# A projection whose sum stays on chip: three of four windows of x1 are kept for the next layer, the first part of x is loaded in the last attention head, and the last two outputs get buffers of their own

## The chip, the core and the metric

The kernel runs on one core of a Trainium2 chip. The core has five engines that run beside each other, each with its own instruction queue: PE (matmuls, with weight loads shown as PEld), DVE (vector work), ACT (pointwise functions and copies), POOL and SP. In this kernel SP does nothing but issue transfers (DMAs); ACT and POOL issue some too. An engine works through its queue in order: an instruction that waits holds back all that stand behind it. Tiles live in the on-chip memory (SBUF, 128 partitions) or in the matmul output memory (PSUM); `dram.tile` is scratch in the chip's main memory. The metric is the time of one execution on the device, in microseconds (us).

## What is computed

One image of 48 channels, 256 x 256, float32, goes through two layers. Cut to what matters:

```python
# layer 0: attention over 4x4 patches, 8 heads, then a 48x48 projection, added to x
qkv = dwconv3x3(einsum('bchw,oc->bohw', gn(x), w_qkv), w_dw)
q, k, v = (heads(unfold4x4(t)) for t in split(qkv, 3))        # 8 heads, 96 x 4096 (+ border)
attn = softmax(einsum('bhcn,bhcm->bhnm', l2norm(q), l2norm(k)) * temperature)
out = fold4x4(einsum('bhcn,bhnm->bhcm', v, attn))
x1 = x + einsum('bchw,oc->bohw', out, w_proj)
# layer 1: on windows of 64 x 64, a sum of three products over width, height and channel
y = gn(x1)                                # group norm: 16 groups of 3 channels, over the whole image
result = x1 + sum_t einsum('bchw,wW,hH,cC->bCHW', window(y), Ws[t], Hs[t], Cs[t])
```

The group norm of x1 needs a mean and a variance over the whole image, so layer 1 cannot begin with a window before the last row of x1 is known.

## The kernel before

**Attention (lines 521 to 715, up to 3318 us of the span).** Heads are worked one after the other, each in 16 steps `g` of two blocks of 128 queries. A step computes two blocks of scores (L344), their exponentials on ACT (L563), and four groups of weighted sums, `weigh` (L592), which DVE adds to `oacc` (L603); meanwhile DVE and ACT prepare the next head (depthwise convolution, in the pool `cv`). In the last head there is no next one, so DVE and ACT have less to do there. In the last step of a head, `store(h, m)` turns the finished sums: PE transposes (L609) into a PSUM tile `pt` (two buffers), ACT copies that into `oo` (L611, two buffers), and POOL writes `oo` with two DMAs (L613) to the scratch `os_`. So the copy of `m` has to wait until both DMAs of `m - 2` have landed. The order of the instructions on every engine is the order of the program text here (`tc.manual_schedule()`).

**Projection (L722 to L781).** x1 is made in eight tiles of 16 rows from the upper and 16 rows from the lower half of the image: channels of the upper half in partitions 0 to 47, of the lower half in 48 to 95. For each tile SP loads two pieces of `os_` (`pot`, L733) and two of x (`pxt`, L734), 768 KB each. PE multiplies by `wp`, a 96 x 96 matrix with `w_projT` twice on its diagonal (L739, eight matmuls of 512 columns in four PSUM tiles `pps`, three buffers). DVE adds the four PSUM tiles to `pxt` (L746) and takes statistics of each pair of rows (`bn_stats`, L750, eight times). POOL writes the tile to the scratch `x1s` (L755). `pot` and `pxt` have three buffers each, so a load of x waits until the write of the tile three before has landed. A scheduler, not the text, orders this part. Then `group_stats` (L761) and a second chain for a 112-partition copy of the variance (`rstd2`, L762 to L767) scale the matrix `csn` (L775); `cbias` (L781) holds what the mean contributes.

**Layer 1 (L784 to L916), in the text's order.** There are eight units: four windows of 64 rows (`yw`) by two halves of the columns (`xh`). For a unit, SP loads `lxq` (L808), the 48 channels of 32 rows in partitions 0 to 47 and of the other 32 rows in 64 to 111, and `lrt` (L817), the same values with rows in the partitions. Both come from `x1s`. `over_c` (L834) multiplies by `csn` in 11 steps of up to three rows, each of which DVE moves from PSUM (`pa`, two buffers) to `lzt` (L841). `over_w` (L856) and `over_h` (L873) do width and height; ACT copies between them (L863), DVE adds the result to `lrt` (`residual`, L885), POOL writes it to the output (L888). The over_c of unit 0 runs alone; the over_c of unit u + 1 is spread over unit u, two steps after each `over_w`, and `over_h` follows after both `over_w` of a third of the unit (`q`).

Every DMA instruction of SP and ACT carries one of eight semaphores in turn and waits, before it is issued, until the DMA that used the same one before it (eight DMAs earlier on the two queues together) has landed. DMAs of POOL have eight others.

Of the kernel before, what the change touches and what calls it, by code (L numbers as in the profile page):

```python
# [16 lines left out]
C = 48  # L17
# [27 lines left out]
def conv_preact_kernel(  # L45
# [36 lines left out]
    make_identity(nc, ident)  # L82
    ones = const.tile([C, 128], F32, name="ones")
# [9 lines left out]
    wp = const.tile([P2, P2], F32, name="wp")  # L93
    nc.vector.memset(wp, 0.0)
    for s in range(2):
        r = slice(s * C, (s + 1) * C)
        for h in range(NH if s == 0 else H0):
            o = s * M0 + h * HC if h < H0 else (h - H0) * HC
            nc.scalar.dma_start(
                out=(wq[r] if h < H0 else wr[0:C])[:, o : o + HC].rearrange("c (z e) -> c z e", z=3),  # L100
                in_=w_qkvT.rearrange("c (z h e) -> h c z e", z=3, h=NH)[h],
            )
        nc.scalar.dma_start(out=wp[r, r], in_=w_projT)
# [22 lines left out]
    mean1 = const.tile([P2, 1], F32, name="mean1")  # L126
    rstd1 = const.tile([P2, 1], F32, name="rstd1")
# [7 lines left out]
    def group_stats(st, mean, rstd, pool, pspool):  # L135

        mv = pool.tile([P2, 2], F32, name="mv")
        nc.vector.bn_aggr(mv, st.rearrange("p n s -> p (n s)"))
        pm = pspool.tile([P2, 1], F32, name="pm", tag="pstat")
        nc.tensor.matmul(pm, lhsT=gm, rhs=mv[:, 0:1], start=True, stop=True)  # L140
        nc.vector.tensor_copy(mean, pm)
        d = pool.tile([P2, 1], F32, name="gsd")
        nc.vector.tensor_sub(d, mv[:, 0:1], mean)
        e = pool.tile([P2, 1], F32, name="gse")
        nc.vector.scalar_tensor_tensor(e, d, d, mv[:, 1:2], ALU.mult, ALU.add)
        pv = pspool.tile([P2, 1], F32, name="pv", tag="pstat")
        nc.tensor.matmul(pv, lhsT=gm, rhs=e, start=True, stop=True)
        f = pool.tile([P2, 1], F32, name="gsf")
        nc.vector.tensor_scalar_add(f, pv, EPS)
        g = pool.tile([P2, 1], F32, name="gsg")  # L150
        nc.scalar.activation(g, f, AF.Sqrt)
        nc.vector.reciprocal(rstd, g)
        return mv, e
# [255 lines left out]
    with tc.tile_pool(name="xn", bufs=1) as xnp, tc.tile_pool(name="cst", bufs=1) as cst, tc.tile_pool(  # L409
# [19 lines left out]
        group_stats(st0, mean0, rstd0, cst, nps)  # L429
# [48 lines left out]
    cv = attention.enter_context(tc.tile_pool(name="cv", bufs=1))  # L478
# [42 lines left out]
    with tc.tile_pool(name="ahead", bufs=2) as ah, tc.tile_pool(name="ae", bufs=3) as ae, tc.tile_pool(  # L521
        name="asm", bufs=6
    ) as asm, tc.tile_pool(name="ao", bufs=1) as ao, tc.tile_pool(name="big", bufs=3, space=PSUM) as big:
        MB = 8
# [80 lines left out]
        def store(h, m):  # L605
# [4 lines left out]
            oo = asm.tile([HD, 512], F32, name="oo", bufs=2)  # L610
            nc.scalar.copy(oo, pt.rearrange("p i n -> p (i n)"))  # L611
            for i in range(512 // TP):
                nc.gpsimd.dma_start(  # L613
                    out=os_[m * (512 // TP) + i, h * HD : (h + 1) * HD, :], in_=oo[:, i * TP : (i + 1) * TP]
                )
# [16 lines left out]
        with tc.manual_schedule():  # L632
            load_query(0, 1)
            block = scores(0, 0)
            for h in range(NH):
                more = h + 1 < NH
                rows = {r: Depthwise(h + 1, r) for r in range(CR + 1)} if more else {}
                for g in range(NG):
                    p, d, n = rows.get(g - 2), rows.get(g - 1), rows.get(g)

                    if h == 0 and 0 < g <= 6:
# [40 lines left out]
                    for k in range(NK):  # L682
# [28 lines left out]
                        if g == NG - 1 and k > 0:  # L711
                            for m in range(2 * k - 2, 2 * k):
                                store(h, m)
            for m in range(6, 8):
# [5 lines left out]
    RP = TP // PX * KS  # L720
    NP = TP
    with tc.tile_pool(name="pj", bufs=3) as pj, tc.tile_pool(name="pjs", bufs=1) as pjs, tc.tile_pool(  # L722
        name="pps", bufs=3, space=PSUM
    ) as pps, tc.tile_pool(name="pp1", bufs=1, space=PSUM) as pp1:
        st1 = pjs.tile([P2, HALF * W // 512, 6], F32, name="st1")
        ov = os_.rearrange("t (c k) n -> t c k n", k=KK)
        for t in range(HALF // RP):
            ot = pj.tile([P2, KK, NP], F32, name="pot")
            xt = pj.tile([P2, RP, W], F32, name="pxt")
            for s in range(2):  # L730
                r = slice(s * C, (s + 1) * C)
                y0 = s * HALF + t * RP
                nc.sync.dma_start(out=ot[r], in_=ov[s * (NT // 2 // TP) + t])  # L733
                nc.sync.dma_start(out=xt[r], in_=xc[:, y0 : y0 + RP, :])  # L734
            xv = xt.rearrange("p (py ki) (px kj) -> p ki kj py px", ki=KS, kj=KS)
            for ki in range(KS):
                ps = pps.tile([P2, KS, NP], F32, name="pps")
                for i in range(0, KS, 2):
                    nc.tensor.matmul(  # L739
                        ps[:, i : i + 2, :],  # L740
                        lhsT=wp,
                        rhs=ot[:, ki * KS + i : ki * KS + i + 2, :],
                        start=True,
                        stop=True,
                    )
                nc.vector.tensor_add(  # L746
                    xv[:, ki], ps.rearrange("p k (py px) -> p k py px", py=RP // KS), xv[:, ki]
                )
            for i in range(0, RP, 2):
                nc.vector.bn_stats(  # L750
                    st1[:, (t * RP + i) // 2, :], xt[:, i : i + 2, :].rearrange("p a b -> p (a b)")
                )
            for s in range(2):
                y0 = s * HALF + t * RP
                nc.gpsimd.dma_start(out=x1s[:, y0 : y0 + RP, :], in_=xt[s * C : (s + 1) * C])  # L755

        gm2 = pjs.tile([P2, 64 + C], F32, name="gm2")
        nc.vector.memset(gm2, 0.0)
        for o in (0, 64):
            nc.vector.tensor_copy(gm2[:, o : o + C], gm[:, 0:C])  # L760
        mv1, e1 = group_stats(st1, mean1, rstd1, pjs, pp1)  # L761
        pc1 = pp1.tile([64 + C, 1], F32, name="pc1", tag="pstat")  # L762
        nc.tensor.matmul(pc1, lhsT=gm2, rhs=e1, start=True, stop=True)
        rstd2 = l1c.tile([64 + C, 1], F32, name="rstd2")
        nc.vector.tensor_scalar_add(rstd2, pc1, EPS)
        nc.scalar.activation(rstd2, rstd2, AF.Sqrt)
        nc.vector.reciprocal(rstd2, rstd2)  # L767
# [190 lines left out]
```

## Time and profile before

| what | value |
|---|---|
| time of three runs | 3765.82, 3767.5, 3774.27 us (median 3767.5) |
| the profiled execution's own time | 3774.41 us |
| its span, first to last instruction | 3772.6 us, 100069 instructions |
| PE, DVE, ACT busy in the span | 3521.1, 2185.9, 1715.5 us (93%, 58%, 45%) |
| 0 to 3288 us (all but the end of the last head) | PE busy 3138.4 us, DMA share 0.44, 111 GB/s |
| 3288 to 3475 us (end of attention, projection, statistics) | PE busy 97.4 us, granted clock 0.69, DMA share 0.91, 221 GB/s |
| 3475 to 3773 us (layer 1) | PE busy 285.4 us, granted clock 0.95, DMA share 0.70, 123 GB/s |

Times in the views are us from the span's start. "DMA share" is the mean busy share of the core's 16 DMA engines; GB/s is what they moved. The chain of waits follows the work that ended last back from the last instruction, at each step to what released it. Lines such as L746 are lines of the kernel before. An fp32 matmul shows as two records.

### The profile page before, as it was taken

The page shows a single profiled execution, that of the slowest core. Times are in us where ns is not written, and L with a number is a line of the kernel's source. Part 1 is how long each engine was busy: PE and PEld are TensorE (multiplying, and loading weights), DVE is VectorE, ACT ScalarE, POOL GpSimd, SP SyncE. Part 2 cuts the span into 40 slices and gives each one's busy share as a digit, 9 for nine tenths or more (in the row PEclk, how much of TensorE's full clock was granted, in tenths as well). Part 3 has the DMA queues.
Part 4 walks back from the last instruction along what each step waited for, and adds up shares of the span by engine and source line. Part 5 has one row for each costly group of instructions (what it writes and reads, how often), then busy time and mean ns, then how long its engine had stood idle before and what let it go on. Part 6 is the DMA issues. An engine that isn't in the chain of part 4 may idle for free.

```text
span 3772.6 us, 100069 instructions
## 1 busy us (share of the span) xinstructions
PE 3521.1 (93%) x44252; PEld 2916.8 (77%) x44252; DVE 2185.9 (58%) x3514; ACT 1715.5 (45%) x2667; POOL 597.5 (16%) x593
## 2 busy tenths in 40 slices
PE   1877999999999999999999999999999999955998
PEld 0335777788888888888888888888888888812776
DVE  5463675169727962896299439934992222256664
ACT  0224565555545554555455445545554444300222
POOL 0031121012301220122122112211221100010011
PEclk9988999999999999999999999999999999966999
DMA  6575666534433542354245424542543100199784
GB/s 144 170 172 159 178 192 177 166 111 118 114 83 99 126 113 73 104 125 107 84 106 122 101 77 113 119 104 75 125 114 93 46 19 23 31 242 199 128 145 91
DMA packets 307826, 441.64 MB, mean 117 GB/s; under 512 B 98474, under 2 KB 232954, under 8 KB 303160
## 3 DMA queue, kind: packets, MB, share of 16 engines
q1 hardware_dynamic: 253668, 269.65, 27.7%
q0 software_dynamic: 48320, 156.61, 18.5%
q10 hardware_dynamic: 5396, 8.88, 1.1%
q8 instruction: 351, 5.75, 0.7%
q14 instruction: 91, 0.75, 0.1%
HBM read 234.76 MB, written 199.95 MB: 115 GB/s over the span
## 4 chain that ended last, share of the span: by engine, by line
PE 84%; DMA 5%; issue 2%; ACT 0%; SPq 0%; DVE 0%; POOL 0%; ACTq 0%; POOLq 0%
PE big L344 37%; PE big L592 36%; PE pb L856 4%; PE pa L834 2%; PE pc L873 2%; PE big L185 2%; DMA x1s<-pxt 1%; DMA pxt<-in_x_dram 1%; DMA t<-ot 1%; PE pt L609 1%; PE pst L546 1%; PE pn L258 1%; DMA kt<-qkv 0%; DMA os__70<-oo 0%; DMA lxq<-x1s 0%
## 5 line engine op out<-in xcount | busy, mean ns | idle before, releaser
L563 ACT ACTIVATE e<-big,nmx 128x1024 f32<-128x1024 f32 x1024 | 1143.9, 1118 | 833.8 <-PE big L344 622.4
L344 PE MATMUL big<-kt,qt 128*128 128x512 f32 x6144 | 1438.9, 393 | 44.4 <-DMA qt<-qkv 31.6
L592 PEld LDWEIGHTS big<-vn,e 128*64 128x64 f32 x32768 | 1365.8, 137 | 83.4 <-ACT e L563 45.1
L592 PE MATMUL big<-vn,e 128*64 128x96 f32 x32768 | 1423.5, 247 | 5.0 <-ACT ot L188 3.1
L344 PEld LDWEIGHTS big<-kt,qt 128*128 128x128 f32 x6144 | 1145.1, 188 | 307.6 <-issue 46.2
L603 DVE TENSOR_TENSOR oacc<-big,oacc 128x768 f32<-128x768 f32 x480 | 458.1, 954 | 708.5 <-PE big L592 708.5
L239 DVE SCALAR_TENSOR_TENSOR acc<-pad,dwt,acc 126x1024 f32<-126x1024 f32 x592 | 766.2, 1295 | 39.1 <-ACT acc L220 23.5
L297 POOL TENSOR_TENSOR ol<-o,oh 126x1024 fp32r<-126x1024 f32 x78 | 187.1, 2399 | 925.3 <-DVE ss L254 800.9
L576 DVE TENSOR_REDUCE zt<-zs 128x1 f32<-128x4 f32 x256 | 38.9, 152 | 360.4 <-ACT e L563 360.4
L563 ACT ACTIVATION_READ_ACCUMULATOR e<-big,nmx 128x1 f32 x1024 | 196.2, 192 | 0.0
L841 DVE TENSOR_TENSOR lzt<-pa,cbias 128x864 f32<-128x864 f32 (+1 forms) x88 | 137.0, 1628 | 96.9 <-PE pa L834 96.9
L863 ACT COPY lyt<-pb 128x512 f32<-128x512 f32 x144 | 84.5, 586 | 212.9 <-PE pb L856 212.9
L302 POOL DMA_DIRECT2D qkv<-o x72 | 88.6, 1230 | 517.6 <-DVE zu L578 248.9
L613 POOL DMA_DIRECT2D os__70<-oo x128 | 65.2, 515 | 599.6 <-ACT oo L611 598.9
L250 ACT ACTIVATE sq<-acc 126x1024 f32<-126x1024 f32 x74 | 78.2, 1057 | 156.3 <-issue 111.1
L284 DVE TENSOR_TENSOR o<-acc,y 126x1024 f32<-126x1024 f32 x74 | 147.6, 1995 | 0.0
L856 PEld LDWEIGHTS pb<-wsb,lzt 128*64 128x64 f32 x2304 | 125.8, 138 | 27.6 <-issue 19.5
L856 PE MATMUL pb<-wsb,lzt 128*64 128x128 f32 x2304 | 141.7, 279 | 1.3 <-issue 1.3
L188 ACT ACTIVATE ot<-big,bias 108x1024 f32<-108x1024 f32 x64 | 71.1, 1112 | 153.7 <-PE big L185 81.4
L739 PE MATMUL pps<-pot,wp 96*96 96x512 f32 x128 | 78.2, 779 | 58.9 <-DMA pot<-os__70 58.9
L220 ACT ACTIVATE acc<-pad,dwt 126x1024 f32<-126x1024 f32 x74 | 84.1, 1137 | 83.0 <-DMA pad<-t 83.0
L318 POOL DMA_DIRECT2D kt<-qkv x44 | 22.9, 527 | 575.8 <-PE big L344 554.5
(116 smaller groups left out, 1904.5 us busy)
## 6 DMA issues: line engine op xcount, KB each, us to landing
pad<-t SPq DMA_DIRECT2D x78, 761.9 KB
qkv<-ol POOLq DMA_DIRECT2D x78, 504.0 KB, 8.9
qkv<-o POOLq DMA_DIRECT2D x72, 504.0 KB, 6.9
qkv<-oh POOLq DMA_DIRECT2D x70, 504.0 KB, 7.4
t<-ot SPq DMA_DIRECT2D x128, 217.7 KB
qt<-qkv SPq DMA_DIRECT2D x176, 96.0 KB
xs<-in_x_dram SPq DMA_DIRECT2D x128, 96.0 KB
os__70<-oo POOLq DMA_DIRECT2D x128, 96.0 KB, 2.1
```

The lines of the kernel that those rows point to most:

```text
L220: nc.scalar.mul(self.acc, self.pad[:, 0:KS, 0:W], dwt[:, self.h, 0:1])
L239: nc.vector.scalar_tensor_tensor(self.acc, self.pad[:, dy : dy + KS, dx : dx + W], dwt[:, self.h, tap : tap + 1], self.acc, ALU.mult, ALU.add,
L284: nc.vector.tensor_tensor(self.o.rearrange("p (a b) x -> p a b x", a=KS), self.acc.rearrange("p a (x b) -> p a b x", b=KS), self.y.rearran ...
L297: eng.tensor_sub(self.ol, self.o, self.oh.bitcast(F32))
L302: eng.dma_start(out=qkv[self.h][i].rearrange("j (c k) n -> (j c) k n", k=KK)[:, :, px], in_=self.o if i == 2 else (self.ol if i else self. ...
L344: nc.tensor.matmul(ps[:, i, :], lhsT=qt[:, r, q0 : q0 + 128], rhs=kts[2 * j + i][:, r // 2, :], start=(r == 0), stop=(r == 2),)
L563: nc.scalar.activation(e[:, j * 1024 : (j + 1) * 1024], ps.rearrange("p a b -> p (a b)"), AF.Exp, bias=nmx[:, b : b + 1], accum_out=zs[:, ...
L592: nc.tensor.matmul(ps[p : p + 64, j // 4, j % 4 * HD : (j % 4 + 1) * HD], lhsT=e[:, mb * 128 + p : mb * 128 + p + 64], rhs=vn, start=(i == 0),
L603: nc.vector.tensor_add(oaccs[h, k], ps[:, :, : 4 * HD], oaccs[h, k])
L841: nc.vector.tensor_tensor(zv[:, :, y0 : y0 + n, :], pa[:, :, : n * T3 * C].rearrange("p s (y k) -> p s y k", y=n), cbias.rearrange("p (u v ...
L856: nc.tensor.matmul(pb[s * WS : (s + 1) * WS, i, :], lhsT=zts[u][:, t * C + c + i, :], rhs=wsb[:, t, :], start=True, stop=True,)
L863: nc.scalar.copy(yt[:, t, :], pb.rearrange("p i x -> p (i x)"))
```

## The change

The changed kernel computes the same. Five things differ, all from the last head on; up to there the instructions of all engines stand in the same order.

1. The pool `cv` lies on the other side of SBUF and is closed at the start of the last head. In its place come `xw`, a tile of x for the whole first window (`xts[0]`: 48 channels of 32 rows in partitions 0 to 47, and of the next 32 rows in 64 to 111), and `pa`. In each of the steps g = 1 to 8 of the last head DVE clears partitions 32 to 63 of four rows and SP loads these four rows (two DMAs of 192 KB). The outputs `oo` of the last two `m` get two buffers of their own in `pa`, and so does the first tile of `os_`.
2. The projection walks by windows: tile t covers the 16-row pieces `sub` of both 32-row halves of window t // 2, in the partitions 0 to 47 and 64 to 111 that layer 1 wants. `wp` is 112 x 64, and each 512-column matmul of 96 x 96 becomes two, of 48 x 64 and 48 x 48. Statistics run over 112 partitions. It stands in the text's order now.
3. The windows' tiles are kept: window 0 in `xw`, windows 2 and 3 in `xk`; window 1 lies in a pool that is given back, is written to `x1s` by POOL and is loaded again during unit 1 (3.1 MB in two DMAs) into the tile of window 0. For windows 1 to 3 ACT clears 32 partitions x 8192 elements before x is loaded. Windows 0, 2 and 3 are still written to `x1s` (for `lrt`), by 12 DMAs of SP that stand behind all loads of the projection.
4. `over_c` reads the kept tiles; `lxq` and its 16 loads are gone. The units' order is window 0, 2, 3, 1. `lrt` is loaded by thirds of a unit into three small buffers. The copy of the variance chain for 112 partitions is gone, since `gm2` now does both.
5. In layer 1 `over_h` stands between the two `over_w` of the following third, and the steps of `over_c` are 2, 2, 2, 2, 3, 0 in place of 2 after each.

```diff
@@ constants, statistics
-    wp = const.tile([P2, P2], F32, name="wp")
+    wp = const.tile([64 + C, 64], F32, name="wp")
...
-        nc.scalar.dma_start(out=wp[r, r], in_=w_projT)
+        nc.scalar.dma_start(out=wp[s * 64 : s * 64 + C, 0:C], in_=w_projT)
@@ attention
-    cv = attention.enter_context(tc.tile_pool(name="cv", bufs=1))
+    convolution = ExitStack()
+    cv = convolution.enter_context(tc.tile_pool(name="cv", bufs=1, side="right"))
...
-            oo = asm.tile([HD, 512], F32, name="oo", bufs=2)
+            oo = (pa if h == NH - 1 and m >= NM - NLATE else asm).tile([HD, 512], F32, name="oo", bufs=2)
...
+        def load_output(ot, t):
+            for s in range(2):
+                nc.sync.dma_start(
+                    out=ot[s * 64 : s * 64 + C],
+                    in_=os_[t // 2 * 4 + s * 2 + t % 2].rearrange("(c k) n -> c k n", k=KK),
+                )
...
+                    if not more and g == 0:
+                        convolution.close()
+                        xw = ctx.enter_context(tc.tile_pool(name="xw", bufs=1, side="right"))
+                        early = ExitStack()
+                        pa = early.enter_context(tc.tile_pool(name="pa", bufs=1, side="right"))
+                        xts[0] = xw.tile([64 + C, 2 * RP, W], F32, name="xwt")
...
+                        if not more and 0 < g <= 2 * RP // 4 and k == 1:
+                            y = slice((g - 1) * 4, g * 4)
+                            nc.vector.memset(xts[0][32:64, y], 0.0)
+                            for s in range(2):
+                                nc.sync.dma_start(
+                                    out=xts[0][s * 64 : s * 64 + C, y],
+                                    in_=xc[:, s * 2 * RP + y.start : s * 2 * RP + y.stop, :],
+                                )
+                        if not more and g == NG - 1 and k == 1:
+                            pots[0] = pa.tile([64 + C, KK, TP], F32, name="pa")
+                            load_output(pots[0], 0)
@@ projection
+        with tc.manual_schedule():
+            for t in range(NTP):
+                w, sub = divmod(t, 2)
+                if t:
+                    pots[t] = pj.tile([64 + C, KK, TP], F32, name="pot")
+                    load_output(pots[t], t)
+                if w:
+                    if sub == 0:
+                        xts[w] = (pjs if w == 1 else xk).tile([64 + C, 2 * RP, W], F32, name="xk")
+                        nc.scalar.copy(
+                            xts[w][32:64].rearrange("p a b -> p (a b)"),
+                            zero[32:64].to_broadcast([32, 2 * RP * W]),
+                        )
+                    load_input(xts[w], w, sub)
...
+                    ps = pps.tile([128, KS, TP], F32, name="pps")
+                    for i in range(0, KS, 2):
+                        for s in range(2):
+                            m = 64 if s == 0 else C
+                            nc.tensor.matmul(
+                                ps[s * 64 : s * 64 + m, i : i + 2, :],
+                                lhsT=wp[s * 64 : s * 64 + C, 0:m],
+                                rhs=pots[t][s * 64 : s * 64 + C, ki * KS + i : ki * KS + i + 2, :],
...
+                if w == 1:
+                    store_x1(w, sub, nc.gpsimd)
+
+            for w in (0, 2, 3):
+                for sub in range(2):
+                    store_x1(w, sub, nc.sync)
@@ layer 1
-        units = [(yw, xh) for yw in range(H // WS) for xh in range(2)]
+        units = [(yw, xh) for yw in (0, 2, 3, 1) for xh in range(2)]
...
-                            lhsT=xq[r, y0 + i, :],
+                            lhsT=xq[r, y0 + i, xcol],
...
-            for u in range(2):
-                load_x(u)
...
-                load_rows(u)
-                if u + 2 < len(units):
-                    load_x(u + 2)
+                if u == 1:
+                    xts[1] = xw.tile([64 + C, HW, W], F32, name="xwt")
+                    for s in range(2):
+                        nc.sync.dma_start(
+                            out=xts[1][s * 64 : s * 64 + C], in_=x1s[:, WS + s * HW : WS + (s + 1) * HW, :]
+                        )
...
                 for q in range(NQ):
+                    load_rows(u, q)
...
-                        for _ in range(2):
+                        for _ in range((2, 2, 2, 2, 3, 0)[2 * q + b]):
                             next(ahead, None)
-                    if late:
-                        over_h(*late)
+                        if b == 0 and late:
+                            over_h(*late)
```

## The prediction, made before the changed kernel ran

> **What bounds the kernel now.** The page's slices come first: PE is busy in nine tenths or more of each slice from the seventh to the 34th, then drops to 5. Everything that the change touches lies there or later; up to the last head the instruction order of no engine changes, so some 3290 us are fixed. Next, the chain of waits from 3270 us on:
>
> ```profile
> 3295.61 5.13 DMA os__70<-oo
> ...
> 3302.29 6.69 DMA os__70<-oo
> ...
> 3346.02 17.16 DMA x1s<-pxt
> ...
> 3363.32 19.82 DMA pxt<-in_x_dram
> ...
> 3451.93 8.46 DMA x1s<-pxt
> ...
> 3461.19 13.87 DMA lxq<-x1s
> ...
> 3475.19 1.79 PE pa L834 x11
> ```
>
> Between the last weighted sum and layer 1 it runs through transfers. Three things are to be seen: two copies `oo` wait 5 to 7 us each for their predecessors' writes; each tile goes round a loop "write x1s, then load x into the same buffer"; and at the end the last write (8.5 us) and its reading back (13.9 us) stand alone. SP's waits from 3290 us on name the loop:
>
> ```profile
> SPq L734 <- DMA x1s<-pxt: 82.8, 7, 17.9
> ```
>
> The timelines of PE, ACT and DVE give the prices:
>
> ```profile
> 3318.17 9.01 PE L739 MATMUL pps<-pot,wp 96*96 96x512 f32 x16 [6.52 <-DMA pot<-os__70]
> ```
>
> ```profile
> 3316.71 0.58 ACT L611 COPY oo<-pt 96x512 f32<-96x512 f32 x1 [3.46 <-DMA os__70<-oo]
> ```
>
> ```profile
> 31.02 4.84 DVE L428 BATCH_NORM_STATS2 st<-xr 96x6 f32<-96x512 f32 x8 [1.21 <-DMA xr<-in_x_dram]
> 38.74 4.84 DVE L428 BATCH_NORM_STATS2 st<-xr 96x6 f32<-96x512 f32 x8 [2.87 <-DMA xr<-in_x_dram]
> ...
> 3356.38 7.62 DVE L746 TENSOR_TENSOR pxt<-pps,pxt 96x1024 f32<-96x1024 f32 x4 [6.42 <-PE pps L739]
> 3363.89 4.85 DVE L750 BATCH_NORM_STATS2 st<-pxt 96x6 f32<-96x512 f32 x8
> ```
>
> A tile costs DVE 7.62 + 4.85, some 12.4 us, but tiles follow every 17.4 us. The first two lines are a stream of nothing but loads of x, 16 KB a partition: two 768 KB loads every 7.45 us on average from 31.0 to 68.2 us, 211 GB/s. In the projection, with writes mixed in, stretches of 20 us give (busy time of PE, PEld, DVE, ACT, POOL, then granted clock, DMA share, GB/s):
>
> ```profile
> 3360.00:3380.00 20.00, 10.53 (x19) 3.44 (x17) 16.12 (x15) 0.00 (x0) 1.03 (x2) 0.74 0.99 251
> 3380.00:3400.00 20.00, 10.54 (x16) 3.55 (x16) 13.15 (x14) 0.00 (x0) 1.03 (x3) 0.66 1.02 276
> ```
>
> The DMA engines are full (0.99, 1.02); PE is half idle and DVE a quarter. Layer 1 behind it is PE alone, at clock 1.00.
>
> **The change part by part.** Times are on the clock of the profiled span; T is the end of DVE's last `bn_stats` of the projection.
>
> *Last head.* Eight clears of 32 x 1024 on DVE: a clear of 384 elements took 0.378 us (L790), so about 1.0 us each. They stand between two `oacc` additions, before each of which DVE sat idle 1.68 us: 0, at most 8 x 1.0 = 8 us without that cover. The 16 loads pass SP behind the step's queries; SP then waits for the clear, and behind it stand the next queries, which wait for PE's next step anyway: 0.
>
> *Start of the projection.* It could start at 3318.17 because the copies went two by two, each pair behind a write (3294.2, 3300.9, 3309.1, 3312.7 and 3316.7). Now no loads of x crowd these writes, and the last two copies wait for PE only. Copies of m 2 and 3 at about 3298 and 3299 (a write without traffic lands in 2.1 us by the issue table), their writes land 5 to 7 us later as before (the first tile's load is under way), m 4 and 5 at about 3305 and 3307, m 6 and 7 right behind, to 3308.6. The first tile's `os_` pieces (1.57 MB), issued from 3297.4, land at about 3306. PE starts at 3308.6 in place of 3318.2, DVE's first addition 3.9 us later as before: 3312.5.
>
> *ACT's clears, a new wait.* 1024 elements took 1.118 us, 512 took 0.586: 1.04 ns an element, 8.6 us for 8192. The first waits for the writes of m 4 and 5 (3313.5), and behind it SP waits with all further loads: 3322.3. The first three tiles of `os_` are issued before that. Tile 2 needs its x at 3337, 14 us later, and one pair takes 7.45: hidden.
>
> *DVE and loads.* DVE alone: 3312.5 + 8 x 12.4 = 3412. Loads: from 3322.3 on, eleven pairs (six of x, five of `os_`), 17.3 MB. By the load stream 11 x 7.45 = 82 us, to 3404.3. POOL's writes of window 1 (3.1 MB) fall in this time: 0 if they pass beside, 11.6 us at 270 GB/s if not; I take 6. The last pair is there at 3410.5; the eighth tile's DVE work adds 12.4, landing 0.6: T = 3423.5. Ends: at the mixed rate of 271 GB/s all 20.4 MB take 75 us, then DVE sets 3412; at the slowest stretch with loads alone (153 and 156 GB/s, below; 10.1 us a pair) T = 3452. I take the stream, the nearest row in kind. Before, T was 3455.87 (3451.02 + 4.85): **-32.4 us**.
>
> ```profile
> 3320.00:3324.00 4.00, 4.00 (x8) 1.46 (x7) 1.94 (x2) 0.00 (x0) 0.00 (x0) 0.74 0.95 153
> 3324.00:3328.00 4.00, 3.18 (x8) 0.98 (x6) 3.96 (x4) 0.00 (x0) 0.00 (x0) 1.00 0.90 156
> 3452.00:3456.00 4.00, 0.00 (x0) 0.00 (x0) 3.97 (x8) 0.00 (x0) 0.45 (x1) 0.50 1.01 205
> ```
>
> [...]
>
> *PE in the projection.* Per tile 16 matmuls of 512 columns in place of 8. If the two halves of the array run at once, the tile stays at 9 to 10.5 us, under DVE's 12.4. Layer 1 shows such packing: `over_h`, 64 x 64, 512 columns, puts 24 records (12 matmuls) into 2.73 us, 0.23 us each, where full-height ones took 13.63 us for 29 records (L158, clock 1.00), 0.94 us each. If not, 16 x 0.94 = 15.0 us at the full clock, 18 to 21 us (twice the rows above) at the projection's clock of about 0.7. By 15.0 us PE would end the last tile at 3429 and DVE 7 us later (an addition and `bn_stats`): T = 3436. I take side by side.
>
> [...]
>
> *From T to layer 1.* Before, 39.6 us lay between T and the first `over_w` (3495.46). The write and its reading back go; what is late next is the statistics' chain, 6.67 us to `cbias`, of which 0.76 (the second variance chain) goes, then 0.4 us of clearing and `over_c` of unit 0, 18.5 us from its first DVE step (3477.00) as before: 24.8 us. **-14.8 us**.
>
> *Writes and residuals.* Twelve writes on SP (9.4 MB) begin behind the last load, 3411. The program makes the eighth and later ones wait for semaphores of `hsb` and `wsb`, issued by ACT only after the statistics (about 3429). At the 205 GB/s that the last write shows above they take 46 us, to 3457, and the first `lrt` lands at about 3460. The first residual needs it 18.2 us after layer 1's start at 3448.3, so 3466.5: hidden by 6 us; 0, at most 10 us at 150 GB/s. Later `lrt` have three buffers and over 20 us of lead.
>
> *Layer 1's order.* Third step in a row: two PSUM buffers `pa`, PE fills one in 0.83 us, DVE empties one in 1.65, so the third fill waits 0.87 us. PE was without a gap here, so 7 units x 0.87 = **+6.1 us** (0 to 8). At the end a second `over_w` now covers the addition that left PE idle 1.3 us (3760.3 to 3761.6): **-1.3 us**. Loading window 1 again (3.1 MB) falls into unit 1 and is needed in unit 5: 0.
>
> *Sum.* -32.4 - 14.8 + 6.1 - 1.3 = -42.4 us. The profiled execution (3774.41, span 3772.6) would be 3732; it stood 6.9 above the median, to which the same difference is applied: 3767.5 - 42.4 = **3725 us**.
>
> **The rivals.**
> - *DVE paces.* Loads at 260 GB/s or more: T = 3412, -54 us, 3713. For it speak the 251 to 276 GB/s above; against it, that these hold a third of writes.
> - *Slow loads.* 160 to 190 GB/s: T up to 3450, 3735 to 3752. For it speak the 153 to 156 GB/s and POOL's writes; against it the early stream.
> - *Slower: PE takes the matmuls one after the other at a low clock.* The whole gain is used up when T is 3423.5 + 42.4 = 3466, that is when a tile takes (3466 - 7 - 3309)/8 = 18.8 us. At 21 us T is 3484, the time 3786. [...] Against: the packing in layer 1, and that a PE so full would not keep a clock of 0.7; at 15.0 us a tile the time is 3737.
> - *The round trip isn't saved.* `lrt` takes the place of `lxq` as what layer 1 waits for; if the writes move at 130 GB/s (72 us, to 3483, `lrt` 3 us later) the first residual waits 20 us: 3745.
>
> **How the numbers follow.** Chances: loads pace as taken, 3718 to 3735, 0.50; DVE paces, 0.20; slow loads or late `lrt`, 0.22; one after the other at a low clock, 0.08. Cases of 3706 to 3752 hold 0.85: that is the range. Its ends are DVE's pace with no third-step wait (3707) and T = 3452 (-4 in place of -32, 3753). A difference under 0.2% (7.5 us) can't be told from none. Faster 0.89, same 0.04, slower 0.07.
>
> **What would show it.** First projection matmul at 3306 to 3312; no wait for `x1s<-` on SP's loads, DVE tiles 12.4 us apart at first and 14 to 16 later, waiting for loads of x or `os_`; `over_c` of unit 0 within 7 us of the last statistics; `pa` waiting for `lzt` once per unit. Wrong would be: 32 projection records taking over 15 us, loads under 160 GB/s, a first residual waiting for `lrt`, or PE gaps in the last head.

## The result and the profile after

| | before | after |
|---|---|---|
| median, lowest to highest of 12 runs each | 3772.02 us (3765.82 to 3781.12) | 3771.48 us (3763.63 to 3786.99) |
| ratio of the medians, 95% interval | 1 | 1.000 (0.9985 to 1.0014) |
| profiled execution: span | 3772.6 us | 3771.9 us |
| T, the last statistics of the projection | 3455.9 us | 3453.9 us |
| from T to the first `over_w` | 39.6 us | 25.6 us |
| from the first `over_w` to the end of the span | 277.1 us | 292.4 us |

The prediction was 3725 us; it was wrong. The three lower rows add up to the spans: -2.0 - 14.0 + 15.3 = -0.7 us. One of the two large terms, the shorter way from T to layer 1, came as predicted. The other, a projection that ends 32 us sooner, came to 2 us, and layer 1 lost what had been won. In what follows, lines such as L804 are those of the changed kernel.

The chain of waits of the changed kernel from the last head to T (start, duration, what):

```profile
3292.88 8.37 DMA os__70<-oo
...
3302.73 17.85 DMA os__70<-oo
...
3322.06 5.38 DMA os__70<-oo
...
3327.62 7.03 ACT xk L792
...
3337.01 31.68 DMA xk<-in_x_dram
...
3368.70 41.19 DMA xk<-in_x_dram
...
3409.91 31.54 DMA xk<-in_x_dram
```

No `x1s<-` and no `lxq` stand in it any more, so the change does what it says. But the waits for `os_` writes, 5 to 7 us each before, are 8.4, 17.9 and 5.4 us now, and after them 104 us of the chain are loads of x. SP's own waits that end from 3290 us on (total, times, longest) no longer show the 82.8 us for `x1s` writes of the kernel before. Of the 69.5 us for `os_` writes, the 50.3 cost nothing: they begin in the last head, when SP has nothing else to issue, and end at the first load of `os_` (3293.0). The four others come to 19.2 us.

```profile
SPq L639 <- DMA os__70<-oo: 69.5, 5, 50.3
SPq L633 <- DMA xk<-in_x_dram: 29.4, 7, 5.8
```

The timelines of ACT, PE and DVE (start, duration, what, idle time before in brackets and what ended it) show how late the start is and what the tiles wait for:

```profile
3312.06 0.58 ACT L616 COPY oo<-pt 96x512 f32<-96x512 f32 x1 [10.12 <-DMA os__70<-oo]
3327.62 20.85 ACT L792 COPY xk<-zero 32x8192 f32<-32x8192 f32 x3 [4.59 <-DMA os__70<-oo]
```

```profile
3323.12 9.50 PE L804 MATMUL pps<-pa,wp 48*64 48x512 f32 x32 [0.72 <-issue]
```

```profile
3368.81 7.70 DVE L811 TENSOR_TENSOR xk<-pps,xk 112x1024 f32<-112x1024 f32 x4 [4.24 <-DMA xk<-in_x_dram]
3376.42 4.83 DVE L817 BATCH_NORM_STATS2 st<-xk 112x6 f32<-112x512 f32 x8
```

PE starts at 3323.1 us, 5 us later than before and 14.5 later than predicted. The 32 records (16 matmuls) of the first tile take 9.5 us, those of the third and fourth 10.4 and 11.3, and DVE takes 7.70 + 4.83 us a tile; neither sets the pace. What does is seen in these stretches (busy time of PE, PEld, DVE, ACT, POOL, then granted clock, DMA share, GB/s):

```profile
3335.00:3365.00 30.00, 23.95 (x78) 6.72 (x74) 29.57 (x33) 14.76 (x3) 1.03 (x2) 0.77 1.02 155
3365.00:3395.00 30.00, 15.24 (x36) 3.72 (x36) 15.30 (x14) 0.00 (x0) 1.03 (x2) 0.68 0.99 251
3395.00:3414.00 19.00, 14.27 (x40) 3.65 (x36) 13.56 (x14) 0.00 (x0) 0.00 (x0) 0.68 1.01 194
```

The DMA engines are full (share 1.0) while they move 155 GB/s in the first of these stretches. From the first load of window 1 (3334.67) to the landing of the last pair (3441.45) eleven pairs take 106.8 us, 9.7 us a pair in place of 7.45.

In layer 1 PE's waits from 3470 us on, and the lines around the longest, are

```profile
PE pa L883 <- DVE lzt L890: 7.6, 10, 1.0
PE pa L883 <- issue: 6.6, 1, 6.6
```

```profile
3524.64 1.00 PE L883 MATMUL pa<-csn,xk 48*128 48x144 f32 x10
3532.25 2.05 PE L883 MATMUL pa<-csn,xk 48*128 48x144 f32 x13 [6.61 <-issue]
```

Three of the ten waits of the first line, 0.7 us, belong to the `over_c` of unit 0; the other seven, 6.9 us, are the third step in a row, as predicted. The second line is new: in the middle of a step PE stands still for 6.6 us with nothing in the profile that it waits for. Before, all waits of PE from 3490 us to the end came to 2.8 us. PE's busy time in layer 1 is 270.4 us, 2.8 more than before.

### The profile page after: what moved, and what is told of

Read it like the earlier page. It is cut to its first block, busy times and chain, and to the rows that moved or that the text cites. A ratio compares the mean times of both kernels' runs of the same rounds, so it can differ in the third digit from the quotient of the medians.

```text
span 3771.9 us, 100412 instructions
## 1 busy us (share of the span) xinstructions
PE 3533.1 (94%) x44378; PEld 2915.3 (77%) x44378; DVE 2190.9 (58%) x3519; ACT 1736.0 (46%) x2669; POOL 590.3 (16%) x581
## 4 chain that ended last, share of the span: by engine, by line
PE 79%; issue 6%; DMA 5%; POOL 1%; DVE 1%; ACT 0%; SPq 0%; POOLq 0%; ACTq 0%; DVEq 0%
PE big L346 37%; PE big L597 37%; DMA xk<-in_x_dram 3%; PE big L187 2%; DMA os__70<-oo 1%; PE pst L551 1%; PE pb L905 1%; PE pt L614 1%; PE pn L260 1%; PE pa L883 1%; POOL out_dram L937 1%; DMA kt<-qkv 0%; DMA vt<-qkv 0%; PE pc L922 0%; DMA t<-ot 0%
## 5 line engine op out<-in xcount | busy, mean ns | idle before, releaser
L230 PE MATMUL dps<-pad,diag 126*126 126x512 f32 x216 | 98.3, 616 | 13.9 <-DMA pad<-t 13.9
```

The lines of the kernel that those rows point to most:

```text
L230: nc.tensor.matmul(ps[:, i, :], lhsT=diag[:, tap, :], rhs=self.pad[:, y : y + 2, dx : dx + W], start=(tap == 0), stop=(tap == 8),)
```

## The experiments

Each kernel ran beside runs of the kernel before on the same chip; ratios are against those.

### The pace of the loads: transfers alone

Theories at this point: the place in memory, the partitions, the queue, or the work beside the loads makes a pair take 9.7 us. The first kernel of transfers alone:

```diff
+    load("one queue, 0 and 48, halves", 48, (SP, SP), lambda i, s: xc[:, halves(i, s), :])
+    done()                     # DVE reads one column of each of the 8 tiles
+    load("one queue, 0 and 64", 64, (SP, SP), from_x)
+    done()
...
```

> Leaves the whole computation out and only moves data: stages of sixteen transfers of 768 KB (48 partitions of 16 KB), each stage behind a read of the one before. In order: x from one queue into partitions 0 and 48; x from one queue into 0 and 64; the same two from two queues (SP and ACT); writes of the scratch in the layout of os_ from 0 and 64; the scratch from one queue into 0 and 64; x into partition 0 for both halves; into 0 and 64 with DVE adding beside; into 0 and 64 once more; writes by POOL. Theory (the partitions set the pace): 0 and 48 moves at about 211 GB/s, 0 and 64 at 160 to 195 on one queue and on two. Rival (one queue in place of two): both layouts 160 to 195 on one queue, both 210 or more on two. Second rival (loads are slow only beside other work): all stages near 211, the one with DVE beside it 155 to 195. Third (the scratch): only the stage from the scratch is slow.

It settled little. `done()` lets each tile go as soon as it was read, so the loads on ACT's queue of the third stage ran during the second one. The second stage, 100.6 us for eight pairs, thus carried foreign traffic too. What it did show: x into 0 and 64 at 144 to 164 GB/s with DVE adding beside it, and no stage of loads from x alone on one queue at the 211 GB/s that the prediction had used. The second kernel put a clear of all tiles behind the reads:

```diff
     def done():
         for i in range(8):
             nc.vector.tensor_copy(acc[:, i : i + 1], ts[i][:, 15, 255:256])
+        for i in range(8):
+            nc.vector.memset(ts[i][:, :, 0:1], 0.0)
```

> Again only transfers of 768 KB, sixteen a stage, now with a clear between the stages that each next transfer waits for, so that no stage runs into another (in the first such run the second queue ran ahead). Stages: x on one queue into partitions 0 and 48 (1) and 0 and 64 (2); on two queues 0 and 48 (3), 0 and 64 (4); writes to the scratch in the layout of os_ (5) and of x1s (6); one queue from os_ (7), from the x1s scratch, 256 KB from channel to channel as in x (8), and from x taken as 48 neighbouring runs of 16 KB (9); os_ and x by turns on one queue (10), os_ on SP and x on ACT (11), by turns with each pair split over both (12); stage 2 with DVE adding beside it (13). Theory (where in memory the 48 runs lie sets the pace, not the partitions or the queues): stages 1, 2, 8 within 10% of each other at 150 to 190 GB/s, 7 and 9 at 220 to 240, 10 between them at 185 to 200; two queues help stages 3, 4, 11, 12 by under 10%. Rival A (partitions): stage 2 at least 15% slower than 1, and 4 than 3. Rival B (one queue): 3, 4, 11 and 12 at least 15% faster than 1, 2 and 10. Rival C (work beside the loads): 13 at least 10% slower than 2.

Where each pair lands is seen from DVE's copy that waits for it. The first and last of stages 1 and 2:

```profile
50.73 0.15 DVE L90 COPY acc<-t 128x1 f32<-128x1 f32 x1 [10.75 <-DMA t<-in_x_dram]
...
108.09 0.15 DVE L90 COPY acc<-t 128x1 f32<-128x1 f32 x1 [7.35 <-DMA t<-in_x_dram]
...
121.88 0.15 DVE L90 COPY acc<-t 128x1 f32<-128x1 f32 x1 [13.41 <-DMA t<-in_x_dram]
...
194.04 0.15 DVE L90 COPY acc<-t 128x1 f32<-128x1 f32 x1 [10.32 <-DMA t<-in_x_dram]
```

Seven pairs take 57.4 us into 0 and 48 and 72.2 us into 0 and 64: 8.19 and 10.31 us a pair, on one queue. Read in the same way: two queues, 0 and 48, 7.34 us; two queues, 0 and 64, 7.78; from the x1s scratch 10.22; from 48 neighbouring runs 9.44; os_ and x by turns on one queue 10.14; os_ on SP and x on ACT 11.1; by turns with each pair divided over both queues 8.28. With DVE adding beside it the rate in GB/s was 156, against 146 without. So my theory (the place in memory) fell: the x1s scratch and x, and os_ by turns with x, differ by under 2%, and neighbouring runs gain only 8%. DVE is out as well. Rival A (partitions) holds on one queue, by 26%, and not on two (6%); rival B (one queue) holds for 0 and 64, by a third, and not for 0 and 48 (12%). The loads from os_ alone don't fit: they took 6.9 to 7.0 us a pair but for the last two, the 220 to 240 GB/s that my theory had said for them. They had started while the writes of the stage before were still under way, yet kept that pace for 40 us behind the last of these (429.4 us), so that stage stays open. The kernel takes os_ and x by turns, and that stage took 10.14 us.

Note what stage 3 is: two queues and partitions 0 and 48, just as the early stream of x in the prediction, and its 7.34 us (7.75 without the last pair, behind which nothing queues) are near that stream's 7.45.

The stages of the third kernel, all with the same rows of x as their source:

```diff
+            SP.dma_start(out=ts[i][0:C], in_=rows(i, 0))              # stage 3, eight times
+            SP.dma_start(out=ts[i][64 : 64 + C], in_=rows(i, 0))      # stage 4
+            SP.dma_start(out=ts[i][32 : 32 + C], in_=rows(i, 0))      # stage 5
...
+                for k in range(16 // n):                              # stages 6 and 7: n = 8, 4
+                    for s in range(2):
+                        SP.dma_start(out=ts[i][64 * s : 64 * s + C, k * n : k * n + n], in_=rows(i, s, n, k))
```

> Transfers alone, a clear between the stages, all x from the same rows. Stages on SP's queue: 0 and 64 (1); 0 and 48 (2); eight transfers into 0 to 47 (3), eight into 64 to 111 (4), eight into 32 to 79 (5); 0 and 64 in pieces of 8 rows (6) and of 4 rows (7) by turns; then 0 and 64 with SP and ACT (8), with SP and POOL (9), with POOL alone (10). Theory (a transfer into one half of the partitions is limited by that half, and one queue sends the halves one after the other): 1 takes about 10.3 us a pair and 2 about 8.2 though their sources are now the same; 3 and 4 take about 5.1 us a transfer, 5, across both halves, about 3.9 or less; 8 and 9 take under 8 us a pair. Rival (it was the rows of x that differed between those stages): 1 and 2 within 5%, 3, 4 and 5 alike. Whether smaller pieces mix the halves is open: 6 and 7 at 8 us if so, at 10.3 or more if not.

The windows of stages 1 to 8, from the first landing to the last (seven pairs, in stages 3 to 5 seven single transfers; columns: busy time of DVE and POOL, granted clock, DMA share, GB/s):

```profile
53.40:124.50 71.10, 1.01 (x8) 0.00 (x0) 1.00 0.97 148
136.10:194.40 58.30, 0.99 (x8) 0.00 (x0) 1.00 0.97 180
203.10:243.10 40.00, 1.00 (x8) 0.00 (x0) 1.00 0.94 126
251.60:289.50 37.90, 0.95 (x8) 0.00 (x0) 1.00 0.93 133
295.60:317.70 22.10, 0.97 (x8) 0.00 (x0) 1.00 0.93 225
330.30:396.90 66.60, 0.96 (x8) 0.00 (x0) 1.00 0.98 159
407.00:456.90 49.90, 0.98 (x7) 0.00 (x0) 1.00 1.01 214
470.30:535.00 64.70, 1.00 (x8) 0.00 (x0) 1.00 0.97 162
```

Divided by seven: 10.2 us a pair into 0 and 64, 8.3 into 0 and 48, though the source is the same. One transfer of 768 KB takes 5.7 us into 0 to 47, 5.4 into 64 to 111, and 3.2 into 32 to 79, which reaches over partition 64. The DMA share is 0.93 to 0.94 in all three, at 126, 133 and 225 GB/s: here it doesn't tell the rate. Pieces of 4 rows by turns bring the same partitions from 10.2 to 7.1 us on one queue; pieces of 8 rows hardly do (9.5). Small pieces without the turns were not run, so what the turns do apart from the size is not shown. SP with ACT took 9.3 here and 7.78 in the run before, so dividing over two queues is not dependable; SP with POOL took 8.1 and POOL alone 10.7 (the first five pairs behind the first landing, 626.2 to 679.8 us).

What in the partitions makes this difference no run shows; its size is 5.7 / 3.2 = 1.8 between a transfer into 0 to 47 and one into 32 to 79. A pair of stage 1 (10.2 us) is close to the two halves one after the other, 5.7 + 5.4 us. A pair of stage 7, by turns in small pieces, takes 7.1 us, less than that sum, and moves 42% faster than in stage 1.

### The same two remedies in the kernel

```diff
         def load_input(xt, w, sub):
             for s in range(2):
-                nc.sync.dma_start(
+                (nc.scalar if s else nc.sync).dma_start(
```

and in the same way the loads of `os_` from the second tile on.

> The changed kernel with each pair of the projection's loads divided between the queues of SP (partitions 0 to 47) and ACT (64 to 111); the first os_ tile stays on SP. Theory (a pair is slow because one queue sends both halves one after the other into the same half of the partitions: 10.1 us a pair by the stage that takes turns, 8.3 us divided over two queues): from the first addition to T it takes 105 to 112 us instead of 127 (118.6 and 129.7 in the two runs with the same projection), T about 3438, the time 13 to 18 us under before, 3752 to 3758. Rival (in the kernel the pace is set by the writes of window 1, the 48-byte-free mixing of x and os_, or DVE): T - first addition stays between 118 and 130, time within 5 us of before.

Measured 3766.24 us, ratio 0.9985 (0.9970 to 0.9999), 6 us where the theory had 13 to 18. From the first addition (3319.7, 7 us sooner) to T (3444.1) it took 124.4 us: the rival's figure. DVE still waited for x before five tiles, 3.1 to 7.2 us each. So dividing the pairs over two queues does not mend the pace in the kernel, as stage 8 of the third run also says.

```diff
         def load_input(xt, w, sub):
-            for s in range(2):
-                nc.sync.dma_start(
-                    out=xt[s * 64 : s * 64 + C, sub * RP : (sub + 1) * RP], in_=xc[:, image_rows(w, s, sub), :]
-                )
+            for k in range(0, RP, 4):
+                for s in range(2):
+                    y = image_rows(w, s, sub).start + k
+                    nc.sync.dma_start(
+                        out=xt[s * 64 : s * 64 + C, sub * RP + k : sub * RP + k + 4], in_=xc[:, y : y + 4, :]
+                    )
```

and `load_output` likewise, four of the sixteen k at a time.

> The changed kernel with every load of the projection cut into four pieces of 192 KB (4 KB a partition), taken from the two halves by turns, still on SP's queue alone. Theory (on one queue a transfer of 768 KB keeps all engines in one half of the partitions; pieces by turns keep both halves at work): a pair takes 7.1 to 7.5 us as in the run of transfers alone instead of 9.7, so DVE's 12.4 us a tile sets the pace: from the first addition to T 100 to 106 us instead of 127, T 3424 to 3434, time 20 to 28 us under before, 3744 to 3752. The start stays as it is, or comes later, if smaller writes of os_ are crowded more. Rival (in the kernel the writes of window 1 and the mixing of sources hold the pace, as dividing over two queues gave only 6 us): first addition to T 115 us or more, time 3760 or more.

Measured **3737.41 us**, ratio 0.9900 (0.9880 to 0.9920): this one edit brings 37 us against the runs of the kernel before beside it, more than the 20 to 28 expected. T is 3421.0 us; the prediction had said 3423.5. Between the first addition and T lie 106.6 us. In the chain most pairs take 5.7 to 7.0 us (start, duration, what):

```profile
3329.16 7.00 DMA pot<-os__70
3336.18 6.98 DMA xk<-in_x_dram
3343.18 6.98 DMA pot<-os__70
...
3376.11 6.95 DMA xk<-in_x_dram
3383.07 6.64 DMA pot<-os__70
3389.73 6.29 DMA xk<-in_x_dram
```

DVE starts earlier too, which neither theory had expected:

```profile
3314.41 7.89 DVE L814 TENSOR_TENSOR xwt<-pps,xwt 112x1024 f32<-112x1024 f32 x4 [11.78 <-PE pps L807]
```

3314.4 in place of 3326.9 us. In the chain the `os_` writes beside the first loads now take 2.8, 6.4 and 7.5 us, not 8.4, 17.9 and 5.4. The writes and what they wait behind are the same in bytes; only the loads come in smaller pieces.

### The start of the projection

```diff
-        NLATE = 2
+        NLATE = 8
...
-            oo = (pa if h == NH - 1 and m >= NM - NLATE else asm).tile([HD, 512], F32, name="oo", bufs=2)
+            oo = (pa if h == NH - 1 and m >= NM - NLATE else asm).tile([HD, 512], F32, name="oo", bufs=NLATE if h == NH - 1 else 2)
```

The first tile of `os_` then takes a place among the `pot`.

> All eight output copies of the last head get buffers of their own; the first os_ tile is loaded with the others instead of into a place of its own. Theory (the start fails because the copies wait for os_ writes that crawl beside the first os_ loads): the copies end by about 3293 us, the first clear starts there instead of waiting for writes, the first projection matmul comes at about 3311 instead of 3323, the 10 us hole in the transfers at 3325 to 3335 goes, and the end of the statistics T moves from 3453.9 to about 3442 to 3446, since 11 pairs at 9.7 us and three more follow from about 3300. Time 8 to 12 us shorter. Rival (the pace of the loads follows from the work behind them, so a start that comes earlier is given back): T within 3 us of 3453.9, time the same.

Measured 3752.75 us, ratio 0.9955 (0.9939 to 0.9971): 18 us, where 8 to 12 were expected. In ACT's timeline no copy waits for a write any more, and the clears follow right behind:

```profile
3302.97 1.07 ACT L616 COPY oo<-pt 96x512 f32<-96x512 f32 x2 [0.25 <-PE pt L614]
3304.07 20.86 ACT L788 COPY xk<-zero 32x8192 f32<-32x8192 f32 x3
```

They end at 3304, not 3293, because the transposes stand between PE's last weighted sums. The first projection matmul came at 3309.2, but the next, on the other half of the tile, only at 3314.3 (expected 3311 for the first), T at 3435.5 (expected 3442 to 3446). Of the 18 us in T, 9 are the earlier start (first addition 3318.0 in place of 3326.9). The rest is a shorter way from there to T, 117.5 us in place of 127.0; but in the two kernels of the next section, whose projection was left as it was, this way took 118.6 and 129.7 us, so that part proves nothing. The rival, that an early start is given back, is out.

### Layer 1

```diff
-                        for _ in range((2, 2, 2, 2, 3, 0)[2 * q + b]):
+                        for _ in range(2 if 2 * q + b < 5 else 0):
                             next(ahead, None)
                         if b == 0 and late:
                             over_h(*late)
+                        if (q, b) == (NQ - 1, 0):
+                            next(ahead, None)
```

> Of the three steps of over_c in a row, the third is put behind over_h, so that PE has 2.7 us of other work while DVE empties the buffer. Theory (the third step is what layer 1 lost): the seven to eight waits of pa for lzt of 1.0 us in the middle of a unit go, and layer 1 from the first over_w to the end takes about 285 us instead of 292.4. Rival (PE is slowed by something else in layer 1, the 7.6 us of waits move elsewhere): 291 us or more, with the waits under another name. The 6.6 us pause of PE at 3525 us, which neither explains, stays.

PE's waits from 3450 us on:

```profile
PE pa L883 <- issue: 5.9, 1, 5.9
...
PE pa L883 <- DVE lzt L890: 1.3, 5, 0.3
```

One run, 3757.8 us; T came 7.7 us sooner than in the changed kernel with the same projection, so the time itself says little. Layer 1 took 284.2 us in place of 292.4 (from 3471.8 to the span's end at 3756.0): the theory's 285. The waits went, and did not come back elsewhere; the pause stayed.

```diff
-                if u == 1:
+                if u == 3:
                     xts[1] = xw.tile([64 + C, HW, W], F32, name="xwt")
```

> Window 1 is loaded again in unit 3 instead of unit 1. Theory (the pause of 6.6 us at 3525 us, in which PE waits for nothing the profile shows, is an instruction load held up by the 3.1 MB of this transfer): the pause goes from unit 1, or moves with the transfer into unit 3. Rival (it belongs to a place in PE's program, or to chance): a pause of 6 to 7 us at the same instruction with no transfer beside it, or one at an unrelated place.

SP's and PE's timelines with the transfer in unit 3:

```profile
3574.90 1.08 SPq L952 DMA_DIRECT2D xwt<-x1s  x2
```

```profile
3588.60 2.36 PE L922 MATMUL pc<-lyt,hsb 64*64 64x512 f32 x17
3595.56 1.94 PE L922 MATMUL pc<-lyt,hsb 64*64 64x512 f32 x7 [4.60 <-issue]
```

One run, 3780.4 us, with T 9.4 us later than in the changed kernel for the same projection. The pause left unit 1 and stands in unit 3, in another instruction, and again ends 21 us after the transfer's issue; in the changed kernel it was 3509.2 to 3532.3, 23 us, with own buffers 3489.8 to 3509.9, 20 us. So it belongs to the transfer. What PE lacks is less directly shown. The changed kernel's DMA view, in the 23 us before its issue and in the 23 us behind it, lists for the queue that loads instructions (packets, MB, share):

```profile
q8 instruction: 3, 0.05, 1.0%
```

```profile
q8 instruction: 1, 0.02, 0.5%
```

Taken in steps of 1 us, the same view shows more. Between the steps from 3505 and from 3528 us this queue moves no packet, and the packet that ends this gap stands some 4 us ahead of the end of PE's pause (3532.3). With eight pieces, in the first kernel of the next section, it moves nine packets in the 80 us from 3480 us on, and PE has no pause. So in the changed kernel PE goes on shortly after an instruction load that came late. That this packet held PE's instructions is an inference; the profile doesn't say for whom a packet is.

### All together

Own buffers, the third step behind `over_h`, and window 1 loaded again in eight pieces of 4 rows during units 1 to 3:

```diff
                     load_rows(u, q)
+                    y = (u - 1) * NQ + q
+                    if 0 <= y < 8:
+                        for s in range(2):
+                            nc.sync.dma_start(
+                                out=xts[1][s * 64 : s * 64 + C, 4 * y : 4 * y + 4],
+                                in_=x1s[:, WS + s * HW + 4 * y : WS + s * HW + 4 * y + 4, :],
+                            )
```

first with the pairs divided over two queues, and ACT's first clear ahead of them:

> Four edits to the changed kernel together: own output buffers for all eight copies of the last head, each pair of loads divided between SP's and ACT's queues with the first clear ahead of them, the third step of over_c behind over_h, and window 1 loaded again in eight pieces during units 1 to 3. Theory: first projection matmul at about 3313, T about 3420 to 3430 (14 pairs of 8.3 us from 3301 end at 3417, then 12.4 us of DVE), layer 1 in 283 us with neither the waits of 1.0 us nor the pause of PE; together 3728 to 3738, a ratio of about 0.990. Rival (the four overlap: DVE's 12.4 us a tile already sets e1's pace, so dividing the loads adds nothing): T as in the run with own buffers, 3435, and 3742 to 3746.

3731.76 us, ratio 0.9889 (0.9872 to 0.9905), as expected, but in part by luck: T came later than expected and layer 1 was shorter. The first addition came late, at 3329.2: the first tile of `os_` took 18.8 us, with three tiles on their way at once. From there DVE paced almost alone, to T = 3431.2 (expected 3420 to 3430). Layer 1 took 274.8 us (expected 283), with neither the waits nor the pause. Then with pieces by turns on SP's queue in place of the division:

> The four edits together, but with the loads in pieces by turns on SP's queue in place of the division over SP and ACT. Theory: the first os_ tile, 18.8 us on its way when three tiles were divided over two queues, is there after about 9 us, so the first addition comes at 3316 to 3322 instead of 3329; from there DVE paces, 100 us to T = 3416 to 3422; time 3718 to 3726, a ratio of 0.986 to 0.988. Rival (DVE's pace is reached already, and the first tile waits for the os_ writes, not for its own transfer): first addition 3327 or later, time 3728 to 3734.

**3721.01 us**, ratio 0.9853 (0.9835 to 0.9871): 1.5% faster than before, and so than the change, whose ratio is 1.000. The first addition came at 3310.4 us (expected 3316 to 3322), T at 3424.2 (expected 3416 to 3422): DVE waited 11 us for loads in the second half, 7.0 of it here:

```profile
3384.48 7.71 DVE L814 TENSOR_TENSOR xk<-pps,xk 112x1024 f32<-112x1024 f32 x4 [7.00 <-DMA pot<-os__70]
```

Layer 1 took 274.4 us, from 3449.8 on; PE has no wait of its own left in it.

### The pieces without the change

```diff
-                nc.sync.dma_start(out=xt[r], in_=xc[:, y0 : y0 + RP, :])
+                    nc.sync.dma_start(out=xt[r, k : k + 4], in_=xc[:, y0 : y0 + 4, :])
```

in the kernel before, with a loop over k around the two halves, and the same for `pot`.

> The kernel before, its loop of writing x1s and loading x unchanged, with the projection's loads cut into four pieces each, taken from the two halves by turns. Theory (pieces by turns help the changed kernel because its halves lie in 0 to 47 and 64 to 111 and each transfer stays in one of them; the kernel before mixes lower and middle partitions and four streams with writes and is held by the loop): tiles follow every 15.5 to 17.4 us as now, time within 12 us of before, so the changed kernel with pieces (3737) keeps a lead of at least 20 us. Rival (the pieces alone are worth the 34 us, with or without x1 on chip): 3735 to 3745, tiles every 12.5 to 13.5 us.

3756.16 us, ratio 0.9957 (0.9932 to 0.9981): 15 us, a little more than the theory's 12, and not the rival's 34. Tiles follow every 16.4 us on average (3323.07 to 3421.36, six tiles), as the theory said. In the profiles T comes 22 us sooner, at 3433.8: 12.5 of that is the start (first addition at 3309.6 in place of 3322.1), the rest a shorter way from there to T. So by the medians the changed kernel with pieces leads by 19 us (expected 20 or more), by the ratios, each against the kernel before on its own chip, by 21: keeping x1 on chip is worth that, once its loads move.

## Why the prediction was wrong, step by step

- *What bounds the kernel.* Right. The loop through `x1s` went out of the chain, and DMA stayed the bound up to T.
- *Last head.* Right: the clears and the early loads left no mark; the last `vn` of attention came at 3284.1 us, 4 us earlier than before.
- *Start of the projection.* Wrong by 14.5 us: PE at 3323.1, not 3308.6. The step took the `os_` writes to be free of traffic once x was loaded early ("Now no loads of x crowd these writes"), and gave those under the first tile's load 5 to 7 us. But the loads of `os_` that now stand there crowd the writes as much: 8.4 and 17.9 us. With own buffers, or with loads in pieces, the start came 9 or 12.5 us sooner.
- *ACT's clears.* The wait was named rightly; it moved with the writes, so the loads of window 1 began at 3334.7 in place of 3322.3: 12.4 us of the miss. A clear took 7.0 us, not 8.6.
- *DVE and loads.* The step that failed most. A pair was priced at 7.45 us by the early stream of x, "the nearest row in kind". That row had two queues and partitions 0 to 47 and 48 to 95. On one queue into 0 and 64 a pair takes 10.2 us, on two into 0 and 48 it takes 7.3. Eleven pairs took 106.8 us in place of 88 (82 and 6 for the writes): 18.6 us. Together with the 12.4 that is T's miss of 30.4 us, to 0.6 us. Why the partitions matter no run shows. Loads in pieces put T at 3421.0, 2.5 us from the forecast, but that it comes so close is in part luck: this edit also mended the start, and most of its pairs take less than the 7.45 us of the sum.
- *PE in the projection.* Right: 9.5 us for the 32 records of the first tile, 10.4 and 11.3 for the third and fourth, side by side: 16 records of the kernel before, 96 x 96, took 9.0. One after the other would have been 15 us or more by the prediction's estimate (16 x 0.94).
- *From T to layer 1.* Right: 25.6 us (24.8 predicted).
- *Writes and residuals.* Right: no residual waited for `lrt`. The return of window 1 was costed at nothing because it was needed only in unit 5. It cost 6.6 us by standing in the way of something else, by the gap above an instruction load; moving it moves the pause, in eight pieces there is none.
- *Layer 1's order.* +6.1 us predicted, 6.9 measured, and it went with the edit made for it. The 1.3 us at the end were won. The rest of the +15.3 us is, to half a microsecond, the pause and 2.8 us more of busy PE, at a granted clock of 0.97 where it was 0.99.
- *The rivals.* "Slow loads", T up to 3450, was the nearest: its 160 to 190 GB/s hold the 162 that 9.7 us a pair come to, and what put T past its 3450 is the late start. It was held for unlikely beside the early stream, which was the wrong row. No case had a late start, slow loads and a pause in layer 1 together, and the range ended at 3752.

## What to carry to other kernels

A row of the profile prices a transfer only if queue, partitions and neighbours are the same: here a pair of loads from x took 7.3 us on two queues into 0 and 48 and 10.3 on one into 0 and 64. Before a rate is carried over, compare how many queues issued it and which partitions it filled. When a tile's halves lie in 0 to 47 and 64 to 111, load them in small pieces by turns, not one half after the other: here that was worth 37 us in the changed kernel and 15 in the kernel before, whose halves lie in 0 to 95. A transfer that nobody waits for is not free either: behind the 3.1 MB of window 1, needed only in unit 5, PE stood still for 6.6 us, by the gap above because an instruction load came late, and behind eight pieces not at all. Small writes are slower beside large transfers too: up to 17.9 us in the chain beside loads of 768 KB, up to 7.5 beside pieces of 192 KB. So cut a large transfer into pieces.

## What the hardware showed that was not expected

- 768 KB took 5.7 us into partitions 0 to 47, 5.4 into 64 to 111 and 3.2 into 32 to 79, at a DMA share of 0.93 to 0.94 each time.
- A DMA share of 0.93 to 1.01 stood for anything from 126 to 225 GB/s of loads.
- Pieces of 192 KB by turns moved 42% faster than transfers of 768 KB into the same partitions (7.1 against 10.2 us a pair), on one queue.
- Writes of 96 KB stood in the chain for up to 17.9 us beside loads of 768 KB, and for up to 7.5 us beside pieces of 192 KB.
- Behind 3.1 MB in two transfers PE stood still for 3.6 to 6.6 us, a pause that ended 20 to 23 us after their issue in four kernels; in the changed kernel it ended some 4 us behind the first packet of the instruction queue in some 23 us.
